# Folding merged row sums onto half of the partitions before the product with ones, and moving issue steps, in an attention and quantized-convolution kernel

## The chip, the core and the metric

The kernel runs on one core of a Trainium2 chip. The metric is device time in microseconds (us), as a median over runs. One further execution was taken by the hardware profiler; its *span* runs from the first to the last instruction of the program.

The core's engines work side by side, each through its own list of instructions in order: TensorE (PE, with weight loads shown as PEld), VectorE (DVE), ScalarE (ACT), GpSimd (POOL) and SyncE (SP). POOL and SP are used here mainly to issue DMA transfers. Matrix products land in PSUM banks; all else on the chip is in SBUF, with 128 partitions.

## The reference

The input `x` has 4 images of 128 channels and 64 x 64 pixels. First comes an attention layer, then a residual block of two 3 x 3 convolutions with quantized weights:

```python
x_norm = _group_norm(x, norm_w, norm_b)                     # 8 groups
qkv = einsum('oc,bchw->bohw', qkv_w, x_norm) + qkv_b
attn = softmax(einsum('bhid,bhjd->bhij', q, k) * scale)     # 4 heads, d = 32, 4096 pixels
out = einsum('bhij,bhjd->bhid', attn, v)
x = x + (einsum('oc,bchw->bohw', proj_w, out) + proj_b)
...
out = relu(batchnorm(conv3x3(x, lsq_quantize(w1))))
out = relu(batchnorm(conv3x3(out, lsq_quantize(w2))) + x)
```

What the change touches is the softmax's denominator: for each head and each query pixel, the sum of `exp(score)` over all 4096 key pixels.

## The kernel before

**Blocks, steps and halves.** The queries of an image are cut into 8 blocks of 512 columns; with 4 images there are 32 blocks, numbered n = 0 to 31. A block has 32 steps (`kt`), one for each 128 keys. A step has two halves: on the score side a half is a pair of heads (`scores`: four matmuls into one of three PSUM buffers, then one `exp` on ACT into the tile `p`, L430 to L444); on the other side a half is 256 of the 512 query columns (`weights`: four products of `p` with `v`, added up in `acc`, L448 to L458). Half p of a block is half p % 2 of step p // 2, so p runs from 0 to 63.

**Order on PE.** The main loop (L766 to L768) puts three score halves and then three weight halves into the lists, over and over. I call one such round a *group*. Scores are one group ahead of weights. Work that doesn't belong to this stream is hung onto weight halves: `schedule` (L633) makes a list of (half, function), and `side` (L741) calls a function once its half is in the list. `ends[i]` (L636) is the last half of the i-th group of the block: 3i, 3i+1 or 3i+2, as n % 3 is 2, 1 or 0. Work that uses PE is placed at `ends[i]`, between the weights of a group and the next scores; such a place is a *visit*. `visit` (L647) places the two halves of a projection at one end, or, with `split`, at two ends that follow each other, and what empties PSUM one half later. `add(kt, f)` places f after the second half of step kt.

These steps set only the order within each engine's list. An engine starts the next instruction of its list when what that one waits for is there; no clock ties POOL or SP to the step at which a transfer was put into the list.

**Row sums.** DVE adds the `p` tiles of 26 of the 32 steps into the tile `r` (`rsum`, 128 x 4 heads x 512, L469 and L471). The other six (`MOVED`, L427: steps 4, 9, 14, 19, 24, 28) are moved by POOL transfers into `rm` (`msum`), the first as a copy (L464), the others with addition (L466). I call these transfers rm4 to rm28. A `p` tile has nine buffers, so the tile of step kt is written again at step kt + 9.

**The end of a block, spread over the next one** (L655 to L665, functions at L473 to L548): at step 1 `merge` adds `rm` into `r` by a POOL transfer (L492). At `ends[6]` and `ends[7]` (some blocks: both at `ends[5]`, block 1: both at `ends[4]`) `sums` multiplies `r` with a 128 x 32 tile of ones, 8 PE instructions for each 256 columns (`total`, L488; a matmul of these float32 operands shows up as two instructions), and ACT copies the result out of PSUM (L496). `spread` sends it through SP into a 128 x 16 tile, `invert` takes the reciprocal and sends it to DRAM, `gather` brings it back spread over the partitions, `weigh` multiplies it onto the block's output `av`, `project` multiplies by `proj_w` (PE, L544), `store` adds bias and residual and writes to DRAM through POOL.

**Projections for the next image.** While image b is worked on, the chunks of image b + 1 are projected to q, k and v (`project_parts`, L319). Blocks 3, 4, 5, 10, 11, 18 and 19 (`two`) project two chunks each, blocks 6, 7, 12 to 15 and 20 to 23 one each; in a single-chunk block the visits are split. The result leaves PSUM through ACT and DVE (L351, L352) and is stored to DRAM by POOL (L356, L375: `kd`, `qd`, `vd`). `load_k`, `load_v` and `load_q` (L406 to L422) bring it back through SP. A q tile has two buffers, so `load_q` for block n + 1 writes the tile of block n - 1.

**Start and end.** Before block 0 the first chunks of image 0 are projected, with idle matmuls (`keep_warm`) to keep PE busy while x arrives. After the last block come two convolutions over 16 bands of rows (`layer`, L833): `load_band` reads a band through SP, `split_band` makes two parts of it on DVE (L573, L574), PE takes 36 matmuls for each band.

Of the kernel before, what the change touches and what calls it, by code (L numbers as in the profile page):

```python
# [22 lines left out]
P = 128  # L23
# [55 lines left out]
def _fast_body(ctx, tc, x, norm_w, norm_b, qkv_wt, qkv_b, proj_wt, proj_b,  # L79
# [32 lines left out]
    nc.gpsimd.memset(ones, 1.0)  # L112
    worst = const.tile([P, FB // D], F32, name="worst")
# [359 lines left out]
    def finish_parts(n):  # L473
# [9 lines left out]

        def total(r, first, end, cs=slice(0, FB)):
            if "l" not in t:
                t["l"] = psa.tile([P, FB], F32, name=f"l{n}", tag="a")
            for h in range(HEADS):
                nc.tensor.matmul(t["l"][h * D : (h + 1) * D, cs], ones, r[:, h, cs],  # L488
                                 start=first, stop=end)

# [3 lines left out]
        def evacuate():  # L494
            t["ls"] = stage.tile([P, FB], F32, name=f"ls{n}", tag="ls")
            nc.scalar.copy(t["ls"], t["l"])  # L496

        def sums(i):
            total(rsum[n], True, True, slice(i * FB // 2, (i + 1) * FB // 2))
            if i == 1:  # L500
                evacuate()


        def sums_at_once():
            total(msum[n], True, False)
            total(rsum[n], False, True)
            evacuate()
# [13 lines left out]
        def spread():  # L521
            t["lq"] = rpool.tile([P, FB // D], F32, name=f"lq{n}", tag="lq")
            nc.sync.dma_start(out=t["lq"], in_=t["ls"][0:P:D, :])

        def invert():
            t["rq"] = rpool.tile([P, FB // D], F32, name=f"rq{n}", tag="rq")
            nc.vector.reciprocal(t["rq"], t["lq"])
            t["rd"] = dram.tile([HEADS, FB], F32, name=f"rd{n}")
            nc.sync.dma_start(out=t["rd"].rearrange("h (j c) -> (h j) c", c=FB // D), in_=t["rq"])
            nc.vector.tensor_tensor(worst, worst, t["lq"], ALU.add)  # L530
            nc.vector.tensor_tensor(worst, worst, t["rq"], ALU.add)

        def gather():
            nc.sync.dma_start(out=rc, in_=t["rd"].unsqueeze(1).to_broadcast([HEADS, D, FB]))
# [15 lines left out]
        return dict(copy=copy, merge=merge, sums=sums, sums_at_once=sums_at_once, bounds=bounds,  # L550
# [43 lines left out]
    keep_warm(26)  # L594
# [21 lines left out]
    for what, j in (("k", 0), ("q", 0), ("k", 1), ("v", 0), ("k", 2), ("v", 1), ("k", 3), ("v", 2),  # L616
                    ("v", 3)):
        for f in first_chunk(j, what, True):
            f()
        if what == "q":  # L620
            five_v()
            six_v()
        if what == "v" and j < 3:
            load_k(0, j + 1)
# [8 lines left out]
    def schedule(n, before):  # L633
# [21 lines left out]
        if before:  # L655
            add(1, before["merge"])
            e = visit(5 if two else 4 if n == 1 else 6, lambda: before["sums"](0), lambda: before["sums"](1),
                      split=not two and n != 1)
            at_half(e + 2, before["spread"])
            at_half(e + 6, before["invert"])  # L660
            at_half(e + 8, before["gather"])
            at_half(e + 12, before["residual"])
            at_half(ends[18] - 4, before["weigh"])
            at_half(ends[18], before["project"])
            at_half(ends[18] + 2, before["store"])  # L665
        if n + 1 < len(blocks):
# [10 lines left out]
        if n == 1:  # L677
            for i, j in zip((0, 2, 8, 10, 12, 14), range(2, NB)):
                if j > 3:
                    at_half(ends[i - 3], lambda j=j: fetch(0, j))  # L680
                visit(i, *project_parts(0, j, lambda j=j: xin[0, j])["q"], split=False)
        qn = qb if b else qb - 1
        if b + 1 < B:
# [10 lines left out]
            if qn == 2:  # L694
# [3 lines left out]
                at_half(ends[1] + 4, late[b][8])  # L698
# [96 lines left out]
    split_band(*bandlist[2])  # L795
    last["sums_at_once"]()
# [11 lines left out]
    nc.sync.dma_start(out=raw_w, in_=wqd)  # L808
# [599 lines left out]
```

## Time and profile before

| | |
|---|---|
| median of 3 runs | 2569.15 us (2565.08 to 2569.88) |
| the profiled execution's own time | 2569.21 us |
| its span | 2567.4 us |
| first score of the attention | 28.5 us after the start |
| end of the last block's weights | 2250.8 us |
| PE, DVE, ACT, POOL busy | 98%, 83%, 81%, 11% of the span |

The page gives busy times of each engine, a chain of work that ended last (followed back from the last instruction), and groups of equal instructions with their mean duration. A matmul's end is modelled, so PE counts as busy where it may be slowed. The timeline lists instructions in order of time: start, duration, engine, line, operation, tile written <- tiles read, count, and in brackets how long the engine had been idle before it and what ended that. The list of transfers gives for each issuing line the size and the time from issue to landing.

### The profile page before, as it was taken

To read this page: it belongs to the slowest core of one execution; us is meant where nothing else is said; L and a number is where in the kernel's file an instruction comes from. 1 tells how busy PE (TensorE), PEld (TensorE's weight loads), DVE (VectorE), ACT (ScalarE), POOL (GpSimd) and SP (SyncE) were. 2 spreads that over 40 slices of the span, in tenths; PEclk is the share of its full clock that TensorE was granted. 3 is DMA by queue.
4 is the path that set the end of the run, shared out by engine and by line. 5 is a ranking of instruction groups with operands and counts; after the bars stand their busy time and mean duration, and the time that the engine had idled before them with its cause. 6 is when DMAs were issued, how large, how long until landed. Compare 5 with 4: busy or idle time off the path is not lost.

```text
span 2567.4 us, 65010 instructions
## 1 busy us (share of the span) xinstructions
PE 2515.2 (98%) x28696; PEld 1504.3 (59%) x28696; DVE 2137.1 (83%) x1402; ACT 2086.7 (81%) x2278; POOL 282.9 (11%) x462
## 2 busy tenths in 40 slices
PE   8999999999999999999999999999999999999995
PEld 6555555555555555555555555555555555567774
DVE  5889888889988898889988988889999999954345
ACT  5889888998988899999988999989999999911224
POOL 2111111111011111110111111111000011000000
PEclk9999999999999999999999999999999999999997
DMA  6777667688766776797767667896666667645004
GB/s 179 179 187 164 171 176 180 158 202 188 176 151 174 169 167 155 167 222 172 169 167 175 154 154 165 194 202 149 148 137 143 145 147 149 143 87 162 1 1 165
DMA packets 148825, 403.85 MB, mean 157 GB/s; under 512 B 59416, under 2 KB 60184, under 8 KB 119992
## 3 DMA queue, kind: packets, MB, share of 16 engines
q0 software_dynamic: 45984, 280.92, 47.8%
q1 hardware_dynamic: 100680, 113.07, 17.3%
q10 hardware_dynamic: 1872, 5.64, 0.6%
q8 instruction: 227, 3.72, 0.6%
q14 instruction: 62, 0.51, 0.1%
HBM read 107.48 MB, written 56.42 MB: 64 GB/s over the span
## 4 chain that ended last, share of the span: by engine, by line
PE 85%; DMA 6%; issue 4%; DVE 3%; ACT 1%; SPq 0%; POOL 0%; ACTq 0%; POOLq 0%; DVEq 0%
PE s L442 38%; PE acc L456 34%; PE c L781 8%; DMA rm<-p 3%; DVE r L471 2%; PE pk L317 1%; PE l L488 1%; PE po L317 1%; PE pq L317 1%; PE pv L317 1%; DMA t<-y 1%; ACT p L444 1%; DMA rd<-rq 0%; ACT res L946 0%; DMA x<-in_x_dram 0%
## 5 line engine op out<-in xcount | busy, mean ns | idle before, releaser
L444 ACT ACTIVATE p<-s 128x1024 f32<-128x1024 f32 x2048 | 1949.6, 1032 | 216.0 <-PE s L442 161.4
L471 DVE TENSOR_TENSOR r<-r,p 128x2048 f32<-128x2048 f32 x768 | 1758.2, 2289 | 69.4 <-ACT p L444 18.7
L442 PE MATMUL s<-q,k 64*128 64x512 f32 x8192 | 1140.6, 409 | 6.7 <-ACT p L444 5.5
L456 PE MATMUL acc<-p,v 128*32 128x256 f32 x16384 | 1027.1, 383 | 1.0 <-DVE v L371 1.0
L442 PEld LDWEIGHTS s<-q,k 64*128 64x128 f32 x8192 | 715.1, 185 | 417.4 <-issue 167.7
L456 PEld LDWEIGHTS acc<-p,v 128*32 128x32 f32 x16384 | 462.6, 109 | 485.6 <-issue 249.2
L466 POOL DMA_DIRECT2D rm<-p x160 | 139.1, 870 | 848.0 <-ACT p L444 602.7
L848 ACT COPY cv<-c 128x512 f32<-128x512 f32 x60 | 35.2, 587 | 204.1 <-DVE st L847 204.1
L781 PE MATMUL c<-hi,wq 128*128 128x512 f32 x540 | 140.4, 404 | 3.8 <-DVE hi L573 2.5
L781 PE MATMUL c<-lo,wq 128*128 128x512 f32 x540 | 138.6, 401 | 0.0
L847 DVE BATCH_NORM_STATS2 st<-c 128x6 f32<-128x512 f32 x60 | 41.9, 699 | 103.1 <-PE c L781 82.8
L781 PEld LDWEIGHTS c<-hi,wq 128*128 128x128 f32 x540 | 102.2, 190 | 33.4 <-issue 5.0
L781 PEld LDWEIGHTS c<-lo,wq 128*128 128x128 f32 x540 | 101.6, 188 | 27.2
L352 DVE SCALAR_TENSOR_TENSOR kst<-pk,b,kst 128x512 fp32r<-128x512 f32 x32 | 24.0, 750 | 81.3 <-PE s L442 54.9
L469 DVE TENSOR_TENSOR r<-p,p 128x2048 f32<-128x2048 f32 x32 | 73.2, 2288 | 14.9 <-ACT p L444 14.9
L352 DVE SCALAR_TENSOR_TENSOR qst<-pq,b,qst 128x512 fp32r<-128x512 f32 x32 | 24.0, 751 | 71.9 <-PE s L442 59.7
L356 POOL DMA_DIRECT2D qd<-qst x31 | 23.1, 744 | 277.3 <-DVE qst L352 271.1
L492 POOL DMA_DIRECT2D r<-rm x31 | 26.2, 846 | 214.5 <-DMA rm<-p 100.1
L356 POOL DMA_DIRECT2D kd<-kst x28 | 20.8, 744 | 200.1 <-DVE kst L352 189.9
L488 PE MATMUL l<-r,ones 128*32 128x256 f32 (+1 forms) x504 | 37.7, 383 | 0.7 <-DMA r<-rm 0.7
L351 ACT ACTIVATE kst<-pk,b 128x512 fp32r<-128x512 f32 x32 | 22.3, 700 | 18.4 <-PE pk L317 18.4
L317 PE MATMUL pq<-x,wn 128*32 128x256 f32 x480 | 33.3, 379 | 3.9 <-DMA x<-in_x_dram 2.9
(149 smaller groups left out, 725.7 us busy)
## 6 DMA issues: line engine op xcount, KB each, us to landing
rm<-p POOLq DMA_DIRECT2D x192, 1024.0 KB, 7.6
q<-qd SPq DMA_DIRECT2D x248, 128.0 KB
r<-rm POOLq DMA_DIRECT2D x31, 1024.0 KB, 7.6
x<-in_x_dram SPq DMA_DIRECT2D x86, 256.0 KB
k<-kd SPq DMA_DIRECT2D x124, 128.0 KB
qd<-qst POOLq DMA_DIRECT2D x31, 512.0 KB, 7.5
kd<-kst POOLq DMA_DIRECT2D x28, 512.0 KB, 3.8
y<-x POOLq DMA_DIRECT2D x32, 256.0 KB, 7.1
```

The lines of the kernel that those rows point to most:

```text
L317: nc.tensor.matmul(out[cs, :], w[:, cs], x, start=True, stop=True)
L352: nc.vector.scalar_tensor_tensor(lo, ps[what], bias, t[:, 0, :], ALU.add, ALU.subtract)
L356: (nc.sync if start else nc.gpsimd).dma_start(out=dst[b, j].rearrange("s p n -> p s n"), in_=t)
L442: nc.tensor.matmul(s[:, i, :], k[r, half, c0 : c0 + P], q[r, half, part, :], start=(part == 0), stop=(part == 1))
L444: nc.scalar.activation(pts[step][:, 2 * half : 2 * half + 2, :], s, AF.Exp, scale=SCALE)
L456: nc.tensor.matmul(acc[n][h * D : (h + 1) * D, cs], v[:, kt % KB, h * D : (h + 1) * D], pt[:, h, cs], start=(kt == 0 and half == 0), stop= ...
L466: nc.gpsimd.dma_start(out=msum[n], in_=pt, accum_op=ALU.add)
L469: nc.vector.tensor_tensor(rsum[n], pts[step - 1], pt, ALU.add)
L471: nc.vector.tensor_tensor(rsum[n], rsum[n], pt, ALU.add)
L488: nc.tensor.matmul(t["l"][h * D : (h + 1) * D, cs], ones, r[:, h, cs], start=first, stop=end)
L781: nc.tensor.matmul(ps.rearrange("p (r w) -> p r w", w=W), w[:, tap, :], part[:, r0 + kh : r0 + kh + RB, kw : kw + W], start=(n == 0), stop ...
L847: nc.vector.bn_stats(st[:, b * NB + c, :], ps[:, j, :])
```

## The change

The sums of a block are folded first. `merge` stays at step 1. Then three POOL transfers at steps 5, 8 and 11, each of 64 partitions x 2 heads x 512 (256 KB): the first adds the upper 64 partitions of heads 0 and 2 onto the lower 64, the second the lower 64 of heads 1 and 3 onto the upper 64, and the third copies heads 1 and 3 of the upper partitions into the places of heads 0 and 2. After that, one slot holds head 0 in its lower and head 1 in its upper half, another heads 2 and 3. A new tile `pair` has ones for the lower partitions in its first 16 columns and for the upper partitions in its last 16, so four matmuls of 256 columns give the sums of all four heads: half of the PE instructions. They stand in one visit at `ends[9]`. `spread`, `invert` and `gather` are adapted to the new layout, and `gather` is two transfers.

Besides, steps are moved: the end of a block comes later, and in projecting blocks the visits of q come earlier (single-chunk blocks: index 10 becomes 4; `two` blocks: 7 becomes 5, with k from 2 to 3 and v from 9 to 7). Block 1 has its q visits elsewhere, block 0 loses one k chunk, which is projected at the start; six idle matmuls are added there. Loads of the last k and v chunk of an image, of convolution bands and of the second layer's weights stand elsewhere in SP's list.

```diff
+    pair = const.tile([P, D], F32, name="pair")
+    nc.gpsimd.memset(pair, 0.0)
+    nc.gpsimd.memset(pair[: P // 2, : D // 2], 1.0)
+    nc.gpsimd.memset(pair[P // 2 :, D // 2 :], 1.0)
...
+        low, high = slice(0, P // 2), slice(P // 2, P)
+        def fold(i):
+            r = rsum[n]
+            if i == 0:
+                nc.gpsimd.dma_start(out=r[low, 0::2, :], in_=r[high, 0::2, :], accum_op=ALU.add)
+            elif i == 1:
+                nc.gpsimd.dma_start(out=r[high, 1::2, :], in_=r[low, 1::2, :], accum_op=ALU.add)
+            else:
+                nc.gpsimd.dma_start(out=r[high, 0::2, :], in_=r[high, 1::2, :])
+        def sums():
+            l = psa.tile([P, FB], F32, name=f"l{n}", tag="a")
+            for c in range(4):
+                f, i = divmod(c, 2)
+                nc.tensor.matmul(l[c * D : (c + 1) * D, : FB // 2], pair,
+                                 rsum[n][:, 2 * i, f * FB // 2 : (f + 1) * FB // 2],
+                                 start=True, stop=True)
             t["ls"] = stage.tile([P, FB], F32, name=f"ls{n}", tag="ls")
-            nc.scalar.copy(t["ls"], t["l"])
-        def sums(i):
-            total(rsum[n], True, True, slice(i * FB // 2, (i + 1) * FB // 2))
-            if i == 1:
-                evacuate()
+            nc.scalar.copy(t["ls"][:, : FB // 2], l[:, : FB // 2])
...
-            nc.sync.dma_start(out=t["lq"], in_=t["ls"][0:P:D, :])
+            nc.sync.dma_start(out=t["lq"], in_=t["ls"][0 : P : D // 2, : FB // 2])
...
-            nc.sync.dma_start(out=rc, in_=t["rd"].unsqueeze(1).to_broadcast([HEADS, D, FB]))
+            for f in range(2):
+                nc.sync.dma_start(out=rc[:, f * FB // 2 : (f + 1) * FB // 2],
+                                  in_=t["rd"][f].unsqueeze(1).to_broadcast([HEADS, D, FB // 2]))
...
-    keep_warm(26)
+    keep_warm(32)
...
     for what, j in (("k", 0), ("q", 0), ("k", 1), ("v", 0), ("k", 2), ("v", 1), ("k", 3), ("v", 2),
-                    ("v", 3)):
+                    ("k", 4), ("v", 3)):
...
-        if what == "v" and j < 3:
+        if what == "v":
             load_k(0, j + 1)
...
             add(1, before["merge"])
-            e = visit(5 if two else 4 if n == 1 else 6, lambda: before["sums"](0), lambda: before["sums"](1),
-                      split=not two and n != 1)
+            for i, kt in enumerate((5, 8, 11)):
+                add(kt, lambda i=i: before["fold"](i))
+            e = ends[9]
+            at_half(e, before["sums"])
             at_half(e + 2, before["spread"])
-            at_half(e + 6, before["invert"])
-            at_half(e + 8, before["gather"])
-            at_half(e + 12, before["residual"])
-            at_half(ends[18] - 4, before["weigh"])
-            at_half(ends[18], before["project"])
-            at_half(ends[18] + 2, before["store"])
+            at_half(e + 8, before["invert"])
+            at_half(e + 10, before["residual"])
+            at_half(e + 15, before["gather"])
+            at_half(ends[19] - 3, before["weigh"])
+            at_half(ends[19], before["project"])
+            at_half(ends[19] + 1, before["store"])
         if n + 1 < len(blocks):
-            add(24 if n == 0 else 14, lambda: load_q(*blocks[n + 1]))
+            add(22 if n == 0 else 14, lambda: load_q(*blocks[n + 1]))
...
-            for i, what, j in ((0, "k", 4), (2, "k", 5), (4, "v", 4), (6, "k", 6), (8, "v", 5),
-                               (10, "k", 7), (12, "q", 1), (14, "v", 6), (16, "v", 7)):
+            for i, what, j in ((0, "k", 5), (2, "v", 4), (4, "k", 6), (6, "v", 5), (8, "k", 7),
+                               (10, "q", 1), (12, "v", 6), (14, "v", 7)):
...
-            for i, j in zip((0, 2, 8, 10, 12, 14), range(2, NB)):
+            for i, j in zip((1, 3, 6, 11, 13, 15), range(2, NB)):
                 if j > 3:
-                    at_half(ends[i - 3], lambda j=j: fetch(0, j))
+                    at_half(ends[i - 5], lambda j=j: fetch(0, j))
...
-                at_half(ends[1] + 4, late[b][8])
+                at_half(ends[1] + 2, late[b][8])
...
-                    for what, i in dict(k=1, q=10, v=13).items():
+                    for what, i in dict(k=1, q=4, v=13).items():
                         visit(i, *p[what])
                     continue
-                for what, e in (dict(k=2, q=7, v=9) if i == 0 else dict(k=11, q=13, v=15)).items():
+                for what, e in (dict(k=3, q=5, v=7) if i == 0 else dict(k=11, q=13, v=15)).items():
...
         if b > 0 and qb == 0:
-            add(1, lambda: load_kv(b, NB - 1))
+            add(9, lambda: load_k(b, NB - 1))
+            add(16, lambda: load_v(b, NB - 1))
...
-            for kt in (1, 10, 20):
+            for kt in (3, 11, 21):
                 add(kt, lambda: next(pieces, None))
...
-            for kt in (1, 10, 15, 20, 25) + ((29,) if b == 1 else ()):
+            for kt in (3, 12, 17, 22, 26) + ((29,) if b == 1 else ()):
...
     split_band(*bandlist[2])
+    load_band(*bandlist[3])
     last["sums_at_once"]()
...
-    nc.sync.dma_start(out=raw_w, in_=wqd)
...
+        if m == 2:
+            nc.sync.dma_start(out=raw_w, in_=wqd)
         if m == 6:
             nc.vector.tensor_copy(wq[1], raw_w)
-        if m + 3 < len(bandlist):
+        if 0 < m < len(bandlist) - 3:
             load_band(*bandlist[m + 3])
```

The last block's sums (`sums_at_once`) are written differently and do the same work as before.

More of the change, by code (lines that the diff above doesn't have):

```diff
@@ L481, in copy @@
             nc.scalar.copy(av, acc[n])
[L484 to L489, printed above, removed]
         def merge():
             nc.gpsimd.dma_start(out=rsum[n], in_=msum[n], accum_op=ALU.add)
-        def evacuate():
-            t["ls"] = stage.tile([P, FB], F32, name=f"ls{n}", tag="ls")
-            nc.scalar.copy(t["ls"], t["l"])
-        def sums(i):
-            total(rsum[n], True, True, slice(i * FB // 2, (i + 1) * FB // 2))
-            if i == 1:
-                evacuate()
-        def sums_at_once():
-            total(msum[n], True, False)
-            total(rsum[n], False, True)
-            evacuate()
+        low, high = slice(0, P // 2), slice(P // 2, P)
[14 more added lines that the diff above has]
+                                 start=True, stop=True)
+            t["ls"] = stage.tile([P, FB], F32, name=f"ls{n}", tag="ls")
+            nc.scalar.copy(t["ls"][:, : FB // 2], l[:, : FB // 2])
+        def sums_at_once():
+            l = psa.tile([P, FB], F32, name=f"l{n}", tag="a")
+            for r in (msum[n], rsum[n]):
+                for h in range(HEADS):
+                    nc.tensor.matmul(l[h * D : (h + 1) * D, :], ones, r[:, h, :],
+                                     start=(r is msum[n]), stop=(r is rsum[n]))
+            t["ls"] = stage.tile([P, FB], F32, name=f"ls{n}", tag="ls")
+            nc.scalar.copy(t["ls"], l)
             for j in range(4):
@@ L527, in invert @@
             nc.vector.reciprocal(t["rq"], t["lq"])
-            t["rd"] = dram.tile([HEADS, FB], F32, name=f"rd{n}")
-            nc.sync.dma_start(out=t["rd"].rearrange("h (j c) -> (h j) c", c=FB // D), in_=t["rq"])
+            t["rd"] = dram.tile([2, HEADS, FB // 2], F32, name=f"rd{n}")
+            nc.sync.dma_start(out=t["rd"].rearrange("f h (j c) -> (f h j) c", c=FB // D), in_=t["rq"])
             nc.vector.tensor_tensor(worst, worst, t["lq"], ALU.add)
@@ L548, in store @@
             nc.gpsimd.dma_start(out=y0[b][:, qb * FB : (qb + 1) * FB], in_=t["x"])
-        return dict(copy=copy, merge=merge, sums=sums, sums_at_once=sums_at_once, bounds=bounds,
+        return dict(copy=copy, merge=merge, fold=fold, sums=sums, sums_at_once=sums_at_once, bounds=bounds,
                     spread=spread, invert=invert, gather=gather,
```

## The prediction

> **What bounds the kernel now.** I read the page first (chain of work, groups), then the timeline of block 5, then single transfers.
>
> ```profile
> PE 85%; DMA 6%; issue 4%; DVE 3%; ACT 1%; SPq 0%; POOL 0%; ACTq 0%; POOLq 0%; DVEq 0%
> ...
> L488 PE MATMUL l<-r,ones 128*32 128x256 f32 (+1 forms) x504 | 37.7, 383 | 0.7 <-DMA r<-rm 0.7
> ...
> L492 POOL DMA_DIRECT2D r<-rm x31 | 26.2, 846 | 214.5 <-DMA rm<-p 100.1
> ```
>
> The chain is PE's for 85%. The row sums cost PE 37.7 us in all and hardly ever wait (0.7 us): today `merge` lands long before they need it. The 85% don't show how tight PE is; the timeline of block 5 does:
>
> ```profile
> 414.28 1.50 PE L456 MATMUL acc<-p,v 128*32 128x256 f32 x24
> 415.06 0.87 POOL L466 DMA_DIRECT2D rm<-p  x1 [5.73 <-ACT p L444]
> ...
> 417.30 1.50 PE L456 MATMUL acc<-p,v 128*32 128x256 f32 x24
> 418.62 1.05 PE L317 MATMUL pq<-x,wn 128*32 128x256 f32 x16
> ...
> 421.19 1.50 PE L456 MATMUL acc<-p,v 128*32 128x256 f32 x24
> ...
> 423.11 0.70 ACT L351 ACTIVATE qst<-pq,b 128x512 fp32r<-128x512 f32 x1
> ...
> 423.85 0.75 DVE L352 SCALAR_TENSOR_TENSOR qst<-pq,b,qst 128x512 fp32r<-128x512 f32 x1 [3.95 <-PE s L442]
> ...
> 424.89 0.74 POOL L356 DMA_DIRECT2D qd<-qst  x1 [8.97 <-DVE qst L352]
> ```
>
> Three things are to be seen. A group takes 3.02 us (414.28 to 417.30); the median of the 470 groups without a visit is 3.03. A visit of 16 PE instructions adds 0.86 (421.19 - 417.30 - 3.03), one of 8 adds 0.43 (median group 3.46). And qd is issued 6.27 us after pq starts, since ACT takes it behind three more `exp`; counted from the last 8 of pq, 5.84 us, which 27 of the 30 qd of the trace keep (the others take 6.4 to 6.8). Today rm9 goes out at 415.06, long before that qd.
>
> Transfers, from the list of block 5's kd and block 10's vd and rm:
>
> ```profile
> kd<-kst POOLq DMA_DIRECT2D x1, 512.0 KB, 3.3
> ...
> rm<-p POOLq DMA_DIRECT2D x1, 1024.0 KB, 7.0
> vd<-vst POOLq DMA_DIRECT2D x1, 256.0 KB, 2.3
> ```
>
> Taken one by one, a plain 512 KB store with nothing in front lands after 3.25 us, an adding rm alone after 6.9 to 7.4, a rm issued right behind a store 4.75 to 6.7 us *after that store* (median 5.2 to 5.8), a 256 KB store behind a rm 0.6 to 0.7 after the rm. POOL's transfers drain one after another.
>
> The rest is stalls, group by group against those periods: 21.8 us up to the last block's end, 4.2 of it the first fill. Five lie in block 1 and its start (6.1 us), one of 1.1 in block 0, 1.7 in block 10, and 9.4 us around the starts of blocks 8, 16, 24, like this one:
>
> ```profile
> 1725.15 0.73 PE L442 MATMUL s<-q,k 64*128 64x512 f32 x4
> 1727.88 4.69 ACT L444 ACTIVATE p<-s 128x1024 f32<-128x1024 f32 x5 [3.96 <-DMA rm<-p]
> ```
>
> `exp` may not write a `p` tile before rm28 has read it, and rm28 took 12 us beside loads of k and v.
>
> **What the Trainium skill says.** *Perfetto Trace Analysis* (Identifying the Most-Contended Engine): matmul busy time is no measure of how close PE is to its peak; so I use group periods. *DMA: Bandwidth & Descriptors* (Queues, rings and completion order): an engine consumes descriptors in ring order and alternates between queue rows by packets; the additive landings agree. Same page (Anatomy of one DMA): 2.0 us + bytes/436 GB/s, an estimate of 3.2 for 512 KB, trace 3.25; for an adding 1 MB it gives 4.4, trace 7.0, so measurement decides. Same page (Rules for kernel authors): transfers on partition halves spray over the same 16 engines, so I give the folds no path of their own; no run here shows it yet.
>
> **Gains.** *Sums:* 46 visits of 8 and 8 of 16 cost 46 x 0.43 + 8 x 0.86 = 26.7 us; 31 visits of 8 remain, 13.3: minus 13.3. *Block 1:* visits leave the places that waited for `av`, for `merge` and for late x (1.27 + 0.95 + 2.88 + 0.40): minus 5.5. *Block 0:* a k visit fewer (0.86) and v7 earlier (1.08): minus 1.9. *Block 10:* k after the v bias is ready: minus 1.7. *Convolution:* the first band of layer 1 that isn't ready makes PE wait 2.51 us for `hi`, whose band is loaded after `raw_w`; it is now loaded earlier: minus 2.5. Sum: minus 24.9.
>
> **Free edits.** k4 at the start (PE 0.86, DVE 0.75): PE's first scores stand at 28.5 but wait for q until 30.0; uncovered 0.9. Six idle matmuls, 6 x 0.30 = 1.8 us, end near 11.4, before the mean that PE awaits until 12.45; uncovered 1.8. Three memsets of 0.1 us ahead of the first POOL loads, which land 5 us early. ACT's shorter copy: ACT needs 2.86 us of each group. Later `spread`, `invert`, `gather`: `rc` is needed by `weigh` at `ends[19] - 3`, which is 54 to 56, and with sums at 27 to 29 today's 12 us from sums to `rc` (411.7 to about 425) end near half 41; beyond 12 us more they would stop PE at `project`. `gather` as two 128 KB transfers instead of one moves the same bytes, one SP issue of 0.5 us more. `residual` and `store` each issue one transfer and are read a block later. The quantization pieces, each up to five DVE operations of 0.4 to 0.6 us and a 192 KB load, move by one to two steps within blocks that have no projection, moved and not added; DVE has 26 x 2.29 + 2 = 61.5 us of sums and the like in some 65 there. The x loads of block 1 go six halves sooner ahead of their visits, which the gain of block 1 already has.
>
> **The losses: fold 3 stands behind qd and rm9.** In the changed POOL list every block that projects q early has: qd, rm9, fold 3 (fold 1 and 2 before; in blocks with n % 3 = 2 mostly fold 2 after qd). PE's sums wait for fold 3, and behind them on PE are the next scores, so a wait there is a full loss: ACT and DVE run dry after the three halves that they are ahead, and no engine can give the time back to PE. From the last 8 instructions of pq: qd issued 5.84, landed + 3.25, rm9 + 5.2, fold 3 (plain, 256 KB) + 0.7 = 15.0 us. PE gets to the sums four groups later: in a `two` block 4 x 3.03 + 0.43 + 0.86 (v visit) = 13.4, in a single-chunk block 4 x 3.03 + 0.43 = 12.55. Stalls: `two` 1.6 (3, 4, 10, 18, 19: 8.0); with fold 2 between (an adding quarter of a rm, 1.3) and v in front (0.65) 3.55 (5, 11: 7.1); single 2.45 (6, 7, 12, 13, 15, 21, 22: 17.2); with fold 2 between 3.75 (14, 20, 23: 11.3). Together **43.5 us**. With rm9 at 4.75 it is 34, at 6.3 and a slow fold 70. Folds are not in the trace; their price lies between the plain rate (0.65) and twice the adding one (2.6).
>
> Blocks without q: rm9 landed at halves 22 to 27, sums stand at 27 to 29. Only 8 and 16, where rm9 landed at 27, and block 1 are near: 3 us (0 to 6).
>
> *load_q:* in the old list it stood behind `spread` and `invert`, which wait for the sums. With n % 3 = 0 or 1 it now stands before `spread`, and SP runs ahead: it goes when the tile of block n - 1 is free, at half 60 of that block, beside rm28. k7 at step 9 is no later for the same reason. From its landing to the `exp` that writes its tile, rm28 had 2.2 to 6.9 us in most blocks, and it took 7; beside such loads rm took 9.5 in the median. I take plus 6 (minus 5, as v7 leaves the block's start, to plus 20).
>
> *What is late next:* rm9 itself lands some 5 us later than today. Its tile is written again at step 18, and it had 4.5 to 11 us before that; rm14 waits for rm9, and had 5 to 10. The stall at the sums moves those needs back by its own 2 us, so I put nothing here; the cover is thin in block 23 (4.5), and 1 us there is in the range.
>
> *project* has `weigh` one half less ahead; it had 0.5 to 1.8 us to spare in most blocks. DVE catches up while PE stalls: plus 3 (0 to 9).
>
> **Sum.** 2567.4 - 24.9 + 43.5 + 3 + 6 + 3 = 2598 of span; the profiled execution had 1.8 us more than its span and equals the median within 0.1: **2600 us**.
>
> **Rivals.** *The fold lands in time* (faster): needs qd to fold 3 in under 7.6 us (`two`) or 6.7 (single), where the trace has 9.2. Then 2567.4 - 24.9 + 6 + 3 + 1.8 = 2553. It decides from a mean stall of 0.8 us over 17 blocks: (24.9 - 12) / 17. For it: the trace of before has no stall of that kind, with DMA engines idle a third of the time. Against: no landing there is that short. *Starts of blocks pay too* (slower still): rm28 late by 3 to 5 us in a dozen blocks, merges and rm4 late with it: 20 to 40 more, 2625. For it: the 5.0 us at 1725. Against: most rm28 have 4 us to spare. *Nothing changes*, with ACT as the next bound: it works 2.86 us of a group's 3.03, so it has 0.17 x 21 = 3.6 us to give in a block, and the change takes 0.4 to 0.9 of PE's time in one; it would give 2567, and the profile excludes it as the only effect.
>
> **Chances.** Forecast with stalls of 30 to 60 us 0.70; starts of blocks too 0.12; fold in time 0.13; the parts cancel 0.05. A measurement of this kernel tells about 0.2%, 5 us, from no change: faster 0.14, same 0.04, slower 0.82. The likeliest case has 2580 to 2625. The range, 2556 to 2634, leaves out about a tenth on each side: full hiding below, 70 us of stalls with late starts above.
>
> **What would show it.** PE idle before the sums' matmuls, released by DMA r<-r, some 40 us in 17 of 31 places and near none in blocks 24 to 31; qd, rm9 and fold 3 landing in that order; group periods still 3.03; the sums' visit 0.43; block 1 without its stalls; first wait of the convolution gone. I am wrong if fold 3 lands before PE arrives, if rm9 passes qd, or if ACT waits for rm28 more than PE for folds.

## The result and the profile after

The changed kernel takes **2673.93 us** (median of 6 runs, 2664.28 to 2683.57) against 2567.74 us of the kernel before in the same session: a ratio of 1.0413, 95% interval 1.0388 to 1.0438. It is slower, as forecast, but by 106 us where the forecast had 31. The profiled execution has a span of 2671.9 us, 104.5 more than before: the last block's weights end at 2359.3 instead of 2250.8 (plus 108.5), and the convolutions behind them take 312.6 instead of 316.6 (minus 4.0).

From the page of the changed kernel: its span, the chain of work that ended last (shares by engine), the groups of the sums (busy time, mean ns | idle time before them, what ended most of it), and the folds in the list of transfers (count, KB each, median us from issue to landing).

```profile
span 2671.9 us, 64800 instructions
...
PE 73%; DVE 12%; DMA 7%; issue 6%; ACT 1%; POOL 0%; ACTq 0%; DVEq 0%; SPq 0%; POOLq 0%
...
L508 PE MATMUL l<-r,pair 128*32 128x256 f32 x248 | 25.4, 488 | 92.0 <-DVE r L475 33.7
L512 ACT COPY ls<-l 128x256 f32<-128x256 f32 x31 | 11.5, 373 | 101.4 <-PE l L508 101.4
...
r<-r POOLq DMA_DIRECT2D x93, 256.0 KB, 7.2
```

The sums' matmuls had waited 0.7 us before the change; now PE stands idle 92.0 us ahead of them, and ACT runs dry with it (101.4). PE's part of the chain falls from 85% to 73%. The folds, a quarter of `rm` in size, take 7.2 us in the median.

The list of waits of the changed kernel, PE's rows (us in total, times, longest):

```profile
PE l L508 <- DVE r L475: 33.7, 7, 5.4
PE l L508 <- DMA r<-r: 30.8, 11, 5.4
PE l L508 <- issue: 20.1, 4, 7.6
PE po L321 <- DVE av L554: 11.3, 11, 1.7
PE l L508 <- DMA vd<-vst: 7.3, 2, 3.7
```

Four releasers are named for one wait. Which is right shows in single landings: in every block with such a wait, the sums' first matmul starts 0.04 to 0.25 us after fold 3 has landed. "DVE r" cannot be it: DVE had made its last addition to that tile before the merge, which the folds follow. So all four rows of `l` belong to fold 3.

Block 6 as an example, from the timeline of the changed kernel:

```profile
507.80 1.67 PE L446 MATMUL s<-q,k 64*128 64x512 f32 x12
...
509.40 1.50 PE L460 MATMUL acc<-p,v 128*32 128x256 f32 x24
513.51 0.86 POOL L470 DMA_DIRECT2D rm<-p  x1 [7.11 <-DMA rm<-p]
...
515.70 1.08 PE L508 MATMUL l<-r,pair 128*32 128x256 f32 x8 [4.80 <-DVE r L475]
...
516.71 2.93 PE L446 MATMUL s<-q,k 64*128 64x512 f32 x12
516.84 0.37 ACT L512 COPY ls<-l 128x256 f32<-128x256 f32 x1 [5.35 <-PE l L508]
...
519.57 2.39 PE L460 MATMUL acc<-p,v 128*32 128x256 f32 x24
...
521.89 1.67 PE L446 MATMUL s<-q,k 64*128 64x512 f32 x12
```

PE ends the weights at 510.9 and stands until 515.70. And then something that the forecast did not have: the group after the sums (516.71 to 521.89) takes 5.18 us instead of 3.03, its scores 2.93 instead of 1.67 and its weights 2.39 instead of 1.50. The next group is normal again. Windows of the same stretch (busy us of PE, PEld, DVE, ACT, POOL, then the granted PE clock, DMA share, GB/s):

```profile
505.00:507.80 2.80, 2.80 (x36) 1.41 (x34) 2.77 (x2) 2.80 (x4) 1.40 (x2) 1.00 0.96 281
507.80:516.70 8.90, 4.10 (x48) 1.96 (x44) 7.36 (x4) 3.47 (x4) 0.86 (x1) 0.88 0.81 164
516.70:521.90 5.20, 5.20 (x42) 2.81 (x38) 2.77 (x2) 3.23 (x4) 0.00 (x0) 0.55 0.65 128
521.90:525.00 3.10, 3.10 (x42) 1.83 (x38) 1.86 (x2) 2.01 (x3) 0.00 (x0) 1.00 0.01 3
```

The granted clock (the share of full speed that PE is given) is 0.55 in exactly that group. So this wait costs twice: once while PE stands, once while it works at about half clock afterwards.

The transfers of this block, issued between 504.0 and 505.5 (the list cut to that window; us from issue to landing):

```profile
rm<-p POOLq DMA_DIRECT2D x1, 1024.0 KB, 8.1
qd<-qst POOLq DMA_DIRECT2D x1, 512.0 KB, 3.3
r<-r POOLq DMA_DIRECT2D x1, 256.0 KB, 10.0
```

They were issued in the order qd (504.06), rm9 (504.82), fold 3 (505.41) and landed at 507.4, 513.0 and 515.5: one after another.

**Where the 104.5 us are.** I took all groups up to the end of the attention against the undisturbed period (3.03 us, and 0.43 for each visit of 8), sorted them by what stands in them, and subtracted the same for the kernel before:

| | before | after | difference |
|---|---|---|---|
| groups with the sums | 1.2 | 103.0 | +101.8 |
| groups without a visit | 8.0 | 28.2 | +20.2 |
| groups with `project` | 1.4 | 13.6 | +12.2 |
| groups with projections and bias products (k, q, v) | 11.7 | 3.0 | -8.7 |
| halved product, one k visit fewer | | | -14.2 |
| first score at 25.6 instead of 28.5 us | | | -2.9 |
| convolutions | | | -4.0 |

That is 104.4 of 104.5. In "groups with the sums" 98 us are waiting for fold 3 (the page's 92.0 begins only where the last weights are modelled to end), the rest is the sums' own matmuls at a lower clock. The 8.0 of before lie nearly all around the starts of blocks 8, 16 and 24; after the change there is nothing there, and the 28.2 lie in groups right behind a wait at the sums.

### The profile page after: what moved, and what is told of

Read it like the earlier page. It is cut to its first block, busy times and chain, and to the rows that moved or that the text cites. A ratio compares the mean times of both kernels' runs of the same rounds, so it can differ in the third digit from the quotient of the medians.

```text
span 2671.9 us, 64800 instructions
## 1 busy us (share of the span) xinstructions
PE 2535.6 (95%) x28460; PEld 1508.7 (56%) x28460; DVE 2139.0 (80%) x1402; ACT 2081.9 (78%) x2278; POOL 366.1 (14%) x557
## 4 chain that ended last, share of the span: by engine, by line
PE 73%; DVE 12%; DMA 7%; issue 6%; ACT 1%; POOL 0%; ACTq 0%; DVEq 0%; SPq 0%; POOLq 0%
PE s L446 32%; PE acc L460 27%; DVE r L475 10%; PE c L801 8%; DMA r<-r 5%; PE po L321 1%; PE pk L321 1%; ACT p L448 1%; PE l L508 1%; PE pq L321 1%; PE pv L321 1%; DVE qst L356 1%; DMA rm<-p 0%; ACT res L968 0%; DMA vd<-vst 0%
## 5 line engine op out<-in xcount | busy, mean ns | idle before, releaser
L446 PE MATMUL s<-q,k 64*128 64x512 f32 x8192 | 1157.6, 415 | 0.4 <-ACT p L448 0.4
L446 PEld LDWEIGHTS s<-q,k 64*128 64x128 f32 x8192 | 728.8, 188 | 415.6 <-issue 169.5
L867 DVE BATCH_NORM_STATS2 st<-c 128x6 f32<-128x512 f32 x60 | 41.9, 699 | 104.0 <-PE c L801 82.4
L508 PE MATMUL l<-r,pair 128*32 128x256 f32 x248 | 25.4, 488 | 92.0 <-DVE r L475 33.7
L512 ACT COPY ls<-l 128x256 f32<-128x256 f32 x31 | 11.5, 373 | 101.4 <-PE l L508 101.4
L473 DVE TENSOR_TENSOR r<-p,p 128x2048 f32<-128x2048 f32 x32 | 73.3, 2291 | 13.7 <-ACT p L448 12.8
L508 PEld LDWEIGHTS l<-r,pair 128*32 128x32 f32 x248 | 6.7, 121 | 104.4 <-issue 55.0
L360 POOL DMA_DIRECT2D kd<-kst x27 | 20.2, 747 | 242.5 <-DVE kst L356 200.4
```

Of the source, the lines that this page charges most:

```text
L360: (nc.sync if start else nc.gpsimd).dma_start(out=dst[b, j].rearrange("s p n -> p s n"), in_=t)
L446: nc.tensor.matmul(s[:, i, :], k[r, half, c0 : c0 + P], q[r, half, part, :], start=(part == 0), stop=(part == 1))
L473: nc.vector.tensor_tensor(rsum[n], pts[step - 1], pt, ALU.add)
L508: nc.tensor.matmul(l[c * D : (c + 1) * D, : FB // 2], pair, rsum[n][:, 2 * i, f * FB // 2 : (f + 1) * FB // 2], start=True, stop=True)
L867: nc.vector.bn_stats(st[:, b * NB + c, :], ps[:, j, :])
```

## The experiments

The theory: fold 3 waits its turn behind qd and rm9, which POOL issued before it, and PE stands at the sums until it lands (**queue**); the groups behind a wait are slow because the clock was lowered (**clock**). The rivals: the folds are expensive as such (**load**), the moved visits and loads cost the time (**moved steps**), or `qd` alone is what holds the fold up. All runs are compared with the kernel before, run beside them (medians 2567.2 to 2568.4). The last three columns are, in us, the first three rows of the table above for each kernel. They come from one profiled execution each, and that one can lie some us off the median: 5.3 above it for "no folds, `weigh` earlier", 3.9 below it for "folds at 5, 6, 7".

| run | median us | ratio to before (95%) | sums | no visit | `project` |
|---|---|---|---|---|---|
| changed kernel | 2673.9 | 1.0413 (1.0388-1.0438) | 103.0 | 28.2 | 13.6 |
| folds at 5, 6, 7 | 2574.4 | 1.0023 (1.0013-1.0033) | 10.5 | 17.5 | 13.7 |
| q late in single-chunk blocks | 2646.1 | 1.0305 (1.0283-1.0327) | 61.1 | 17.0 | 35.3 |
| no folds, steps as changed | 2566.8 | 0.9992 (0.9983-1.0001) | 0.2 | 7.1 | 17.0 |
| idle matmuls ahead of the sums | 2644.5 | 1.0292 (1.0275-1.0309) | 96.7 | 7.6 | 13.4 |
| folds at 5, 6, 7, `weigh` earlier | 2566.1 | 0.9993 (0.9984-1.0002) | 13.6 | 15.6 | 2.2 |
| no folds, `weigh` earlier | 2551.3 | 0.9938 (0.9922-0.9955) | 0.2 | 12.7 | 0.1 |
| mixed, `weigh` earlier | 2549.1 | 0.9934 (0.9918-0.9951) | 4.1 | 10.3 | 0.1 |
| kernel before with folds only | 2596.0 | 1.0105 (1.0087-1.0123) | 13.2 | 8.6 | 32.3 |
| rm9 behind fold 3 | 2584.6 | 1.0068 (1.0053-1.0082) | 20.5 | 20.2 | 14.4 |
| no folds, `load_q` at 16 | 2554.4 | 0.9947 (0.9934-0.9960) | 0.2 | 0.9 | 8.3 |
| mixed, `load_q` at 16 | 2541.1 | 0.9904 (0.9892-0.9917) | 0.9 | 2.0 | 1.1 |

### Folds ahead of qd and rm9

```diff
-            for i, kt in enumerate((5, 8, 11)):
+            for i, kt in enumerate((5, 6, 7)):
```

> The three folds stand at steps 5, 6 and 7, ahead of qd and rm9 in POOL's list; the same transfers with the same bytes, nothing else changed. Queue theory (the time is lost because fold 3 waits its turn behind qd and rm9): the 98 us of waits at the sums and the 28 us lost in the groups right after them go, what is left is 2673.9 - 98 - 28 = 2548 us (2540 to 2562), which is below the kernel before. Load theory (the folding transfers themselves slow PE, or take DMA time from others): the bytes are the same, so at least 2640. Moved-steps theory (visits of q, loads and weigh at their new places cost the time): at least 2640.

Measured: 2574.4 us, 99.5 less than the changed kernel. The same window of block 6 in this kernel (transfers issued between 482 and 484 us):

```profile
rm<-p POOLq DMA_DIRECT2D x1, 1024.0 KB, 10.3
qd<-qst POOLq DMA_DIRECT2D x1, 512.0 KB, 3.9
r<-r POOLq DMA_DIRECT2D x1, 256.0 KB, 3.2
```

Fold 3, now the first of the three, lands after 3.2 us instead of 10.0. The waits at the sums are gone but for blocks 7, 15 and 23 (2.7, 4.3 and 2.9 us). The queue theory stands, and load and moved steps fall as the main cause: the same bytes, the same visits, and 100 us are gone. Whether fold 3 waits in POOL's own queue, or behind whatever was issued before it to the same DMA engines, is not separated by this run. But 2574 is not the 2548 that I expected, and it is not below the kernel before: 10.5 us stay at those three sums, and 17.5 us in groups without a visit, 15.5 of them in blocks 7, 8, 15, 16, 23 and 24: in each of 7, 15 and 23, seven chunks of k and v are loaded beside the folds.

### No folds at all

```diff
-            for c in range(4):
-                f, i = divmod(c, 2)
-                nc.tensor.matmul(l[c * D : (c + 1) * D, : FB // 2], pair, ...)
+            for i in range(2):
+                cs = slice(i * FB // 2, (i + 1) * FB // 2)
+                for h in range(HEADS):
+                    nc.tensor.matmul(l[h * D : (h + 1) * D, cs], ones, rsum[n][:, h, cs], ...)
...
-            for i, kt in enumerate((5, 8, 11)):
-                add(kt, lambda i=i: before["fold"](i))
```

> All moved steps of the change stay, but nothing is folded: 16 PE instructions on the merged sums in one visit at ends[9], with the layout of before behind it. Queue theory: no wait at the sums, no loss after them, but 31 x 0.43 = 13.3 us of matmuls come back: 2548 + 13 = 2561 us (2550 to 2575). Moved-steps theory: the loss stays, 2640 and more.

Measured: 2566.8 us, in the expected band (2550 to 2575) though above its middle (2561); not to be told from the kernel before. This kernel has 13.3 us *more* of matmuls than the one with folds at 5, 6, 7, and is 7.5 us faster. So the folds, even where they are in time, give back more than the product saves: without them the sums never wait and the groups without a visit lose 7.1 instead of 17.5. DMA engines are busy 0.72 to 0.74 of the time between 500 and 1500 us, with folds 0.78 to 0.79.

### q behind the sums in single-chunk blocks

```diff
-                    for what, i in dict(k=1, q=4, v=13).items():
+                    for what, i in dict(k=1, q=10, v=13).items():
```

> In the ten single-chunk blocks q goes back from index 4 to index 10, behind the sums; folds stay at 5, 8, 11. Queue theory: in these ten blocks fold 3 stands behind rm9 only, as in blocks without q, where the wait is 0 to 2.8 us; of their 52.6 us of waits some 43 go, and with them about 17 us lost in the groups after: 2614 us (2600 to 2630). If rm9 alone holds fold 3 up and qd adds nothing, the waits stay at 4 us and more: 2660 to 2674.

Measured: 2646.1 us, 28 less than the changed kernel where I expected 60. The groups with the sums lose 41.9 us less, 34.6 us of it in the ten blocks themselves; those behind them 11 less. So qd adds to the wait, and rm9 alone makes most of it only in blocks 7 and 23, where PE still stands 5.9 and 5.1 us. What I missed is `project`, which loses 35.3 instead of 13.6. The waits of this kernel:

```profile
PE po L321 <- DVE av L554: 29.2, 20, 4.6
...
DVE av L554 <- DMA rc<-rd: 15.5, 5, 4.5
```

With q behind the sums, DVE takes q out of PSUM before it comes to `invert`, so qd, and rm19 behind it in POOL's list, are issued just ahead of `rd`, the transfer by which `invert` sends the reciprocals to DRAM. From the timeline of block 14 in this kernel:

```profile
1107.23 0.90 POOL L470 DMA_DIRECT2D rm<-p  x1
1108.58 0.34 SPq L544 DMA_DIRECT2D rd<-rq  x1
...
1117.57 0.53 SPq L550 DMA_DIRECT2D rc<-rd  x1
```

`rd` has 8 KB and goes out through SP, yet it lands 9.0 us after its issue, 0.2 us after the 1 MB of rm19 (in the changed kernel, with q early, 2.8 us after its issue). `gather` (`rc<-rd`) waits for that landing, and `weigh` for `gather`, whose last transfer goes out at 54.1 us of the block instead of 48.7. Block 20 shows the same: there `gather` goes out 8.9 us after `rd` instead of 2.5. So the early visit of q, which costs so much at the sums, had been covering `project`; that was no part of my working.

### rm9 behind fold 3

```diff
+            elif kt == 9 and n > 0:
+                held.append((msum[n], pt))
...
                 nc.gpsimd.dma_start(out=r[high, 0::2, :], in_=r[high, 1::2, :])
+                rm, pt = held.pop()
+                nc.gpsimd.dma_start(out=rm, in_=pt, accum_op=ALU.add)
```

> The changed kernel with one transfer in another place: rm9 is issued behind fold 3 (step 11) instead of at step 9; folds stay at 5, 8, 11 and q at its early visits. If rm9 is what holds fold 3 up, fold 3 lands 6.11 (qd's issue) + 3.46 (its landing) + 0.7 to 2 = 10.3 to 11.6 us after pq, before PE arrives (12.5 to 13.3): the waits at the sums fall from 98 to under 15, the 28 us after them go too, and the time comes to 2550 to 2580, with what rm9's later landing costs at step 18. If qd alone is enough to hold it up, the waits stay above 50 us and the time above 2620.

Measured: 2584.6 us, just outside the band, with 20.5 us at the sums (expected: under 15). One transfer moved takes 89 of the 106 us back. So qd alone mostly fits in front of fold 3; it is rm9 on top of it that makes fold 3 late. What stays lies in blocks 5, 11, 14 and 20 (3.5, 2.6, 2.9, 2.3 us), where fold 2 is still behind qd and fold 3 waits for it, in 15 and 23 with their loads of k and v, and in block 1.

### Idle matmuls while PE waits

In the 17 blocks with an early q:

```diff
             l = psa.tile([P, FB], F32, name=f"l{n}", tag="a")
+            if n + 1 in (3, 4, 5, 6, 7, 10, 11, 12, 13, 14, 15, 18, 19, 20, 21, 22, 23):
+                for _ in range(11):
+                    nc.tensor.matmul(l[:, FB // 2 : FB // 2 + P], gavg, gavg, start=True, stop=True)
             for c in range(4):
```

> In the 17 blocks that project q early, 11 idle 128 x 128 matmuls (11 x 0.30 = 3.3 us) on unused columns of the sums' PSUM bank stand ahead of the four of the sums, so that PE works while it waits for fold 3; every wait there is 3.5 us or longer, so they end before fold 3 lands. Clock theory (the 28 us in the groups after the sums are PE at half clock, because it stood idle): waits plus idle matmuls together unchanged, but the 28 us shrink to under 8: 2646 to 2656 us. If the loss after a wait is one of refilling ACT and DVE, it stays: 2668 to 2680.

Measured: 2644.5 us, 1.5 below the band and 29.4 less than the changed kernel although PE has more to do. Block 6 in its timeline:

```profile
509.75 1.50 PE L460 MATMUL acc<-p,v 128*32 128x256 f32 x24
511.18 2.72 PE L508 MATMUL l<-gavg 128*128 128x128 f32 x22
514.47 0.64 PE L511 MATMUL l<-r,pair 128*32 128x256 f32 x8 [0.57 <-issue]
515.04 1.68 PE L446 MATMUL s<-q,k 64*128 64x512 f32 x12
```

and in its windows:

```profile
508.10:515.00 6.90, 6.33 (x70) 4.45 (x66) 6.59 (x4) 3.52 (x4) 0.86 (x1) 1.00 0.75 152
515.00:518.10 3.10, 3.10 (x42) 1.80 (x38) 2.03 (x2) 2.66 (x4) 0.00 (x0) 1.00 1.01 206
```

The clock stays at 1.00, the scores after the sums take 1.68 us instead of 2.93, and the groups without a visit lose 7.6 us instead of 28.2. The waits themselves are as long as before (sums with the idle matmuls 96.7 instead of 103.0). So the second loss is one of the clock; a loss from refilling ACT and DVE would not have gone away.

### Folds alone on the kernel before

```diff
-            e = visit(5 if two else 4 if n == 1 else 6, lambda: before["sums"](0), lambda: before["sums"](1),
-                      split=not two and n != 1)
+            for i, kt in enumerate((5, 6, 7)):
+                add(kt, lambda i=i: before["fold"](i))
+            e = ends[9]
+            at_half(e, before["sums"])
...
-                for what, e in (dict(k=2, q=7, v=9) if i == 0 else dict(k=11, q=13, v=15)).items():
+                for what, e in (dict(k=3, q=5, v=7) if i == 0 else dict(k=11, q=13, v=15)).items():
```

> The kernel before with the folds alone: three folds at 5, 6, 7, four matmuls at ends[9], spread, invert, gather and residual behind them as in the changed kernel, and in blocks that project two chunks the visits of k, q, v at 3, 5, 7, which the sums at ends[9] need; all else as before. The halved product saves 13.3 us; against it stand the folds' waits in blocks 7, 15 and 23 and the groups around them, 10 to 25: 2568 - 13 + 15 = 2570 us (2560 to 2582). Were folding free once its place is right: 2555.

Measured: 2596.0 us, outside what I expected. At the sums it behaves as foreseen (13.2); but `project`, at its old place `ends[18]`, loses 32.3 us, and DVE waits 46.6 us there in all for `rc`. 24.8 of the 32.3 us lie in blocks 9, 15, 23 and 30, and in each of them `rd` lands 0.2 to 0.3 us after an rm issued just ahead of it, 6.7 to 8.2 us after its own issue. With sums at `ends[9]` and `project` at `ends[18]` there is no room for that; so the moved steps of the change seem to make room for what the later sums push back. This run doesn't show it alone, since single-chunk blocks have q behind the sums again, as in the run with q late.

### `weigh` earlier, with and without folds

```diff
-            at_half(ends[19] - 3, before["weigh"])
+            at_half(ends[19] - 6, before["weigh"])
```

on the kernel with folds at 5, 6, 7:

> Folds at 5, 6, 7 as in the run before, and weigh three halves sooner, at ends[19] - 6. The 13.7 us that PE still waits for av at project in that kernel fall to 2 or less, since DVE then takes weigh one group sooner: 2574.4 - 12 = 2562 us (2558 to 2567). If weigh isn't late by its place but by rc's landing, the time stays at 2574.

and on the one without folds:

> Nothing folded (16 PE instructions at ends[9]), and weigh at ends[19] - 6. The 17.0 us at project fall to about 2: 2566.8 - 15 = 2552 us (2548 to 2558), faster than before. If the folds were worth their 13.3 us of matmuls, the folded kernel with the same weigh would be the faster of the two; by what was measured so far, it is slower by 7 to 10.

Measured: 2566.1 and 2551.3 us, both in their bands. In both, the loss at `project` all but goes (13.7 to 2.2, 17.0 to 0.1), so `weigh` was late by its place in DVE's list. Without folds the kernel is 0.6% faster than before; with them it is level with it.

### Folds only where nothing is loaded beside them

The kernel with folds at 5, 6, 7 and the earlier `weigh`, but with the unfolded sums (16 PE instructions, layout of before) in three blocks:

```diff
+        plain = n + 1 in (7, 15, 23)
...
         def fold(i):
             r = rsum[n]
+            if plain:
+                return
```

> Folds at 5, 6, 7 and weigh at ends[19] - 6, but in blocks 7, 15 and 23, where seven chunks of k and v are loaded, the sums are taken unfolded (16 PE instructions). If the folds' load beside those loads is what is left of the loss, the 10.5 us of waits at these three sums go, and most of the 17 us at groups without a visit around them (down to about 9): 2562 - 10.5 - 8 + 3 x 0.43 = 2545 us (2540 to 2556), faster than both kernels. If the waits there come from the loads alone, 2560.

Measured: 2549.1 us, inside the band, 17 less than with folds everywhere. The waits at the three sums are gone (3.0 us in block 4 and 1.0 in block 8 stay). So most of what was left of the loss after moving the folds came from folds and loads of k and v in the same blocks.

### `load_q` behind `spread` again

```diff
-            add(22 if n == 0 else 14, lambda: load_q(*blocks[n + 1]))
+            add(22 if n == 0 else 16, lambda: load_q(*blocks[n + 1]))
```

on the unfolded kernel:

> The unfolded kernel with weigh at ends[19] - 6, and load_q at step 16 instead of 14, so that in every block it stands behind spread in SP's list as before the change. If load_q going early, beside rm28, makes the 12.7 us of waits around the starts of blocks 8, 16 and 24, they fall to 6 to 9: 2546 us (2543 to 2549). If the loads of k and v alone make them: 2551, no difference.

and on the mixed one:

> The mixed kernel (folds at 5, 6, 7 but none in blocks 7, 15, 23; weigh at ends[19] - 6) with load_q at step 16. Likewise 2544 us (2540 to 2547) if load_q makes part of the waits around block starts (10.3 us there), 2549 if it doesn't.

Measured: 2554.4 us, where the kernel with `load_q` at 14 had 2551.3 (intervals overlap: no difference shown, and above the forecast), and 2541.1 us, as forecast, where it had 2549.1. In both profiles the waits around starts of blocks all but go: groups without a visit lose 0.9 instead of 12.7 (from the execution that was 5.3 us above its median), and 2.0 instead of 10.3. In the unfolded kernel a new wait stands against that, 6.8 us at `project` in block 7 of the profiled execution. From its timeline there:

```profile
565.54 4.42 SPq L415 DMA_DIRECT2D k<-kd  x4
570.06 1.09 SPq L419 DMA_DIRECT2D v<-vd  x1
571.25 0.88 SPq L544 DMA_DIRECT2D rd<-rq  x1
...
579.27 0.54 SPq L549 DMA_DIRECT2D rc<-rd  x1
```

`rq` was ready at 565.0, but `rd` went out at 571.25 behind five loads of k and v and took 8.0 us to land, so `rc` was issued at 579.27, and DVE waited up to 12.1 us for it before `weigh`. In the profile of the mixed kernel PE has no such wait. At 0.9904 of the kernel before it is the fastest one here; PE's list of waits has nothing left in the attention that is above 2.4 us:

```profile
PE s L446 <- ACT p L448: 2.4, 6, 0.9
```

## Why the prediction was right in direction and wrong in size

**Right: the loss and its mechanism.** qd, rm9 and fold 3 land in that order in all 17 blocks, PE stands before the sums in the blocks named and not at all in blocks 25 to 28, 30 and 31, and the next scores can't start. Moving fold 3 ahead of the two, or rm9 behind it, takes 99.5 and 89.3 us of the 106 back. Of the 73.9 us by which the span passed the forecast, about 39 are longer waits in the 17 blocks, 25 the slow groups behind waits and the sums' own matmuls at a lower clock, 13 the waits of the other blocks and 9 `project`; against them stand 6 for `load_q`, which did not appear, and some 6 of larger gains.

**Wrong: the size of the chain, "15.0 us from the last 8 instructions of pq".** PE's arrival was right (12.52 and 13.34 us, predicted 12.55 and 13.4). Its other end was not; the means over the 17 blocks:

| step | predicted | measured |
|---|---|---|
| qd issued | 5.84 | 6.11 (5.87 single, 6.46 `two`) |
| qd lands after issue | 3.25 | 3.46 |
| rm9 lands after qd | 5.2 | 6.55 |
| fold 3 lands after rm9 | 0.7 | 1.45 |
| sum | 15.0 | 17.57 |

The waits, counted from these arrivals, are 82.8 us instead of 43.5. The two terms that were mis-sized most are transfers with others beside them. I took rm9 at 5.2, the low end of my own medians (5.2 to 5.8); it came 5.5 to 6.8 us after qd in most blocks and 7.0 to 8.9 in blocks 5, 11, 14, 15, 20 and 23, that is, with fold 2 in between (for which the forecast had added 1.3 in five of these six) or with loads of k and v beside it. Fold 3, which I took at the plain rate of a store, took 0.6 to 2.7. I had worked out "at 6.3 and a slow fold 70" as the bad end, and the truth was beyond it. A wait is the difference of two long times, here 15.5 (the forecast's mean with what it added for fold 2 and v) against about 12.9, so an error of 14% in the chain became one of 90% in the waits. Three smaller slips of the working change nothing: the stalls "with rm9 at 4.75" come to 36 and not 34, "12 us from sums to `rc`" is 13.3 by the times beside it, and the stalls named one by one add up to 22.5 and not 21.8.

**Wrong: "a wait there is a full loss".** It is more than that; the forecast put what follows a wait at nothing, and 28.2 us follow in the groups behind, at a clock of 0.52 to 0.73. The run with idle matmuls settles it. A page of the Trainium skill has it: *TensorE: Matmul & The Clock Gate* (Part 1, and its section on HAM oscillation) says that the clock goes to half after an idle window of about 3.4 us, that the window runs freely, and that each wait for a transfer longer than that has the next work start cold. The trace agrees in the main. By PE's idle time in the profile, the ten waits of 4.4 us and more were each followed by a loss of 1.1 to 2.4 us; of the seven of 3.3 to 3.7 us, five were followed by 1.0 to 1.9 and two (blocks 3 and 4) by none, which a free window allows. But waits shorter than the page's window counted too: those of 2.0 to 2.6 us in blocks 1, 2 and 17 were followed by 1.0 to 1.6 us, and only the one in block 9 by none. There the measurement decides.

**Wrong: blocks without an early q.** Predicted 3 us, measured 15.6 (2.6 in block 1, 2.3 in 2, 2.4 in 9, 2.8 in 17, the rest in 8, 16, 24 and 29). rm9 now lands behind folds 1 and 2 (in block 2, 11.1 us after its issue), and fold 3 behind rm9; I had taken rm9's landing from the kernel before.

**Wrong: `project`.** Predicted plus 3, measured plus 12.2. "One half less ahead" is what `weigh` got, and it was short in every block that projects two chunks, by 1.2 us each. Moving `weigh` three halves up took the loss away, so the sign was right and the size of DVE's lag was not.

**`load_q`: plus 6 predicted, not seen in the changed kernel.** There the loss around starts of blocks went from 8.0 to nothing; that PE's waits at the sums gave rm28 the time is likely, but no run shows it alone. Without those waits the groups without a visit lost 7.1 us in one unfolded kernel and 12.7 in the other, both with `load_q` at 14, against 8.0 before: a cost of plus 6 can't be read from that. With `load_q` behind `spread` again, 0.9 and 2.0 us are left, but the time fell only in the mixed kernel. So the mechanism is supported and its size stays open. What was not tried is the step of k7 and v7 by itself.

**The gains came.** Halved product, block 1's late x, block 0's visits and block 10's bias are as worked out (the sums' visit without a wait is 0.43, and the table's rows give 14.2 + 8.7 + 2.9 = 25.8 with the first score, where 22.4 were predicted without it). The first score comes 2.9 us earlier although the forecast took the six idle matmuls at the start as free: between 12 and 20 us PE's granted clock is 1.00 instead of 0.57. That the six matmuls did it is not shown, since the kernel before with folds only, which lacks them, has its first score at 26.3 us and a clock of 0.79. In the convolutions, the wait of 2.5 us for `hi` is gone, and they are 4.0 shorter; 1.5 of that I can't name.

**Against the rivals:** the rivals of late starts of blocks and of no change failed; "the fold lands in time" is what folds at 5, 6, 7 make of the kernel, and even then it is no gain (1.0023), since the folds' load in blocks 7, 15 and 23 and the later `weigh` take what the product saves.

## What to carry to other kernels

In these runs a transfer that was waited for landed behind the large ones issued shortly before it. So list what is ahead of it, from other engines too (`rd` through SP landed behind POOL's rm), and add their landings, at the values they have with the new transfers there, not at those of the old trace. When two long chains end within 3 us of each other, give the forecast the error of the longer one, not a share of their difference. And where PE is kept busy, a wait can be paid again in the group behind it: here 18 of the 21 waits of 2.0 us or longer were, and none of the four shorter ones.

## What the runs showed of the hardware that I had not expected

- After PE had stood 4.80 us, the granted clock was 0.55 in the next 5.2 us and 1.00 after that; eleven idle 128 x 128 matmuls (2.72 us) in the same gap kept it at 1.00. In the changed kernel PE's clock was lowered (to 0.52 to 0.73) in the group behind 18 of its 25 waits at the sums, once behind one of only 2.04 us, and back at 1.00 one group later each time.
- A small transfer landed with a large one of another engine. In the thirteen kernels profiled, the landing of `rd` (8 KB, through SP) can be told apart 258 times. In 88 of them it was issued 0.5 to 2.5 us behind an rm (1 MB, through POOL), and in all 88 it landed 0.15 to 0.45 us after that rm, 5.3 to 9.2 us after its own issue. In the 79 with no rm under way it took 1.4 us in the median and at most 3.6.
- A plain transfer of 256 KB between partitions 64 to 127 of one tile took 3.0 to 3.4 us from issue to landing in 22 of the 31 times with no other transfer of POOL under way (folds at 5, 6, 7; up to 6.0 in the rest). An adding one of the same size took at least 4.15 us, and never had the way to itself. The median of all folds in the changed kernel, where each has others in front, is 7.2 us.
- Three folds (0.75 MB) per block raised the DMA share by 0.05 to 0.06 between 500 and 1500 us (folds at 5, 6, 7 against none), and the kernel with them was 7.5 us slower although it has half of the sums' matmuls. That the DMA share is the reason is not shown.
